# A bias add of the last image on VectorE instead of GpSimd, a frequency table stored in pairs, and two loads in the other order

## The chip, the core and the metric

The kernel runs on one core of one Trainium2 chip. Time is the device time of one execution in microseconds (us). A core has TensorE (PE, matmuls; PEld is its weight load), VectorE (DVE), ScalarE (ACT), GpSimd (POOL) and SyncE (SP, which here only issues transfers). Each executes its own list of instructions in order, and they wait for each other by semaphores. Transfers run on 16 DMA engines; ACT issues some of them too.

## The reference

The input x has 8 images of 128 x 128 pixels with 96 channels. One layer is computed, in two residual steps:

```python
x = x + conv(layernorm(x))        # a global filter in the frequency domain
t = t + ffn(layernorm(t))         # per pixel, 96 -> 384 -> 96
```

`conv` projects 96 to 192 channels, squares the rectified value, takes a two-dimensional FFT, multiplies by a filter, transforms back and projects to 96 channels. The filter is a mix of three stored ones, each interpolated from a small grid over 128 x 65 frequencies; the weights of the mix are a softmax that depends on the image. `ffn` is

```python
h = relu(q_acc(q_acc(q_mul(x) @ q_mul(W1)) + q_mul(b1)))
y = q_acc(q_acc(q_mul(h) @ q_mul(W2)) + q_mul(b2))
```

where q_mul rounds to an 8-bit float (5 exponent bits) and q_acc to fp16. The second bias, b2, is the one that the change moves.

## The kernel before, in words

Each image b runs through three streams. `before` ("a") loads x in blocks of 16 columns for the statistics (`load_x`, line 903) and transposed for the projection, projects, rectifies, squares, transforms along one axis and stores the result Y in device memory. `spectrum` ("s") goes over 33 groups of frequencies: it loads Y and a piece of the table T (`load_t`, line 1134), weighs T by the image's softmax on GpSimd (tw), builds the filter and the spectrum on PE, multiplies them on VectorE, mixes channels and transforms back on PE, and stores V. `after` ("c") goes over 8 blocks of 16 columns, each of four units (q) of 4 columns, 32 units in all: `load_v` (line 1386) loads the block of x into `t` and the block of V into `vin`; `last` (PE, pk) is the last inverse transform, `residual` (DVE) adds it to t; then come the statistics (bn_stats on DVE, `variance` and `rest` on POOL, a root on ACT and a reciprocal on DVE), the normalised and quantised z, its transposition (pz on PE, zT on ACT), `first` (PE, ph), `accumulated` (ACT, y in fp16), `biased` (DVE, y + b1), `hidden` (h), `second` (PE, po), `put` (ACT, o in fp16), the second bias, the sum with t, and the store.

T is a tensor in device memory, filled at the start of the run (`row_store`, line 783): 2 halves x 64 rows x 65 frequencies x 192 channels in fp32. A group g uses the frequencies g+1 and g+33.

Up to the seventh image the second bias and the sum are done for a whole block on GpSimd (`bias`, `add_up`: 128x1536, L1495 and L1498). For the last image they are done unit by unit: `bias_part` (L1502, 128x384) and `add_part` (L1506), both on GpSimd before. For that image the normalisation also differs: `centre` subtracts the mean on GpSimd (L1416, into vin), `norm` multiplies on VectorE (L1423, z), and `hidden` is split between ACT (two thirds, L1473) and DVE (one third, L1471).

The order of the work is not left to a scheduler of the chip. Every piece is recorded by `at` with what it needs; `in_order` (line 472) goes through them with a cost for each kind (COST), with a place in time for each (WINDOWS by stream and image, OFFSETS by kind), and for some kinds of VectorE with an exclusion against GpSimd (SHARED). It writes one list per engine, and at the end each instruction is tied to the one before it on its engine (PINNED), so that the lists stand as written. `keep_warm` (line 636) puts matmuls on zeros (L642, "warm") ahead of some pieces on PE, as many as WARM says for the image and piece. Two pieces of the end matter below: `second` of a unit is ordered after the four `add_part` of the block two before, because o has two buffers, and `load_v` of a block after the store of the block five before, because t has five.

The transfers are issued by SP in the order in which `in_order` has put them; `load_v` issues two, `load_x` one, `load_t` one.

Of the kernel before, what the change touches and what calls it, by code (L numbers as in the profile page):

```python
# [43 lines left out]
MED = 192  # L44
# [23 lines left out]
WINDOWS = {  # L68
    "a": ((-1497.5, 329.4), (863.1, 879.3), (649, 969.5), (584.6, 116.7), (49.5, 721.3), (910.6, 691.7), (1676.3, 504.2), (2001.5, 512.8)),
    "s": ((23.8, 262.2), (71, 1106.2), (630.6, 311.7), (754.9, 352.4), (629.3, 734.8), (-354.6, 114.4), (713.6, 123.4), (2091.2, 75.3)),  # L70
    "c": ((1077.8, 438.5), (962.8, 173.4), (1098.5, 307), (1684.2, 504.4), (1984, 366.6), (2465, 69), (2244, 686.2), (2737, 1205.9)),
}
OFFSETS = {
    "a_context": -91.63,
# [51 lines left out]
    "a_variance": 33.04,  # L126
    "a_variance_1": 33.04,
    "c_accumulated": -189.82,
    "c_accumulated_8": 12.18,
    "c_add_part_8": -199.88,  # L130
    "c_add_up": -72,
    "c_bias": -208.64,
    "c_bias_part_8": 1548.65,
    "c_biased": -131.17,
    "c_biased_8": 271.9,
    "c_centre_8": 49.3,
    "c_first": -9.52,
    "c_first_8": -1055.54,
    "c_hidden": -106.95,
    "c_hidden_2_8": -971.11,  # L140
    "c_hidden_v_8": 73.57,
    "c_inverse": -43.31,
    "c_inverse_8": 194.44,
    "c_last": -159.45,
    "c_last_8": 67.27,
    "c_load_v": -76.92,
    "c_load_v_8": -73.71,
    "c_measure": 212.19,
    "c_measure_8": -31.7,
    "c_norm_8": -808.2,  # L150
    "c_put8": -62.08,
    "c_put8_8": 1012.64,
    "c_quantise": 163.76,
    "c_quantise_v": 259.01,
    "c_residual": -74.18,
    "c_residual_8": -2157.99,
    "c_rest": -211.52,
    "c_rest_8": 83.6,
    "c_root": 122.39,
    "c_root_8": -0.97,  # L160
    "c_second": -134.92,
    "c_second_8": -285.01,
    "c_store": 507.71,
    "c_store_8": -1049.43,
    "c_store_part_8": 881.57,
    "c_turn8": -248.18,
    "c_turn8_8": 72.63,
    "c_turned8": 91.19,
    "c_turned8_8": 922.13,
    "c_variance": -140.17,  # L170
    "c_variance_8": 771.21,
    "s_alone_t": 386.55,
    "s_alone_x": 26.26,
    "s_alone_z": 209.95,
# [22 lines left out]
    ('a', 1): {('project', 0, 0): 4, ('transform', 0, 2): 7, ('transform', 1, 2): 4},  # L197
    ('s', 1): {('along_w', 1): 6, ('invert', 9, 0): 4},
    ('c', 1): {('second', 7): 4},
    ('c', 6): {('first', 12, 0): 4, ('second', 22): 12, ('second', 23): 8, ('first', 24, 0): 3, ('first', 25, 0): 6, ('second', 26): 3, ('first', 27, 0): 6, ('second', 27): 4, ('first', 28, 0): 3, ('second', 28): 10, ('turn8', 7, 1): 6, ('first', 29, 0): 3, ('second', 29): 11},  # L200
    ('s', 7): {('along_w', 4): 3, ('invert', 15, 0): 5},
    ('c', 7): {('last', 0, 0): 3, ('first', 2, 0): 17, ('first', 3, 0): 17, ('first', 5, 0): 11, ('first', 6, 0): 7, ('second', 6): 8, ('first', 7, 0): 8, ('turn8', 2, 0): 12, ('first', 10, 0): 15, ('first', 12, 0): 20, ('first', 14, 0): 15, ('second', 14): 8, ('first', 15, 0): 8, ('second', 15): 15, ('first', 18, 0): 15, ('first', 22, 0): 3, ('second', 22): 7, ('first', 23, 0): 15, ('last', 6, 0): 3, ('turn8', 6, 0): 11, ('first', 26, 0): 15, ('first', 27, 0): 14, ('last', 7, 0): 6, ('first', 28, 0): 7, ('first', 29, 0): 7, ('first', 30, 0): 7, ('second', 30): 8, ('first', 31, 0): 8, ('second', 31): 11},
}

PINNED = (
# [87 lines left out]
    "s_load_y": (SP, 0.9, 1.25),  # L293
    "s_load_t": (SP, 0.65, 0.576),
    "c_load_v": (SP, 2.1, 4.736),
    "c_bias_part": (POOL, 0.84, 0),
    "c_add_part": (POOL, 0.82, 0),
    "c_store_part": (SP, 0.4, 0.48),
    "s_store_v": (ACT, 0.375, 1),
    "c_store": (SP, 0.4, 1.92),  # L300
# [1 line left out]
    "_load_scales": (SP, 2.4, 5),  # L302
}
QUARTER = {"s_along_w", "s_filters_of", "s_mix_low", "s_mix"}
SHARED = {"a_scale", "c_biased", "a_rate_n", "a_rate_v3", "c_quantise_v", "c_hidden_v"}
INSTR = {
    "a_project": 8, "a_transform": 4, "a_rate_p0": 4, "a_rate_p1": 8, "a_rate_p2": 12, "s_along_w": 96,
    "s_filters_of": 24, "s_mix_low": 96, "s_mix": 96, "s_invert": 4, "c_last": 4, "c_turn8": 8, "c_turn32": 16,
# [37 lines left out]
    return [(NG - 1, 0), (NG, 0), (NG - 1, 1), (NG, 1), (NG + 1, 0)] if r == 0 else [(NG - 1, 0), (NG + 1, 0), (NG - 1, 1)]  # L346


def _constants():

    n = np.arange(128)
    angle = 2 * np.pi * (np.outer(np.arange(L), n) % 128) / 128
    cos, sin = np.cos(angle), np.sin(angle)
    sin[0] = sin[L - 1] = 0.0
    norm = 1 / np.sqrt(128.0)

    middle = 2 * np.pi * np.outer(np.arange(64) - 63.5, np.arange(L)) / 128
    half = np.cos(middle), np.sin(middle)
    half[0][:, L - 1] = 0.0
    turn = np.pi * (127 * np.arange(L) % 256) / 128  # L360
    turn = np.cos(turn), -np.sin(turn)
    weight = np.full((L, 1), 2.0)
    weight[0] = weight[L - 1] = 1.0

    rows = []
    for g in range(NG):
        k = g + 1
        rows += [k, k + 32, 64 + k, 96 + k]
    rows += [32, 96, 0, 64]

    turned = []
    for p in range(NP):
        for cs in range(2):
            for r in range(2):
                for g in (2 * p, 2 * p + 1):
                    turned.append(g + 1 + 32 * r + 64 * cs if g < NG or r == 0 else 64 * (1 - cs))
    out = {
        "F1": np.concatenate([cos, sin[1:-1]])[rows].T * norm,
        "F2": np.concatenate([np.stack([half[0], -half[0]], 1), np.stack([half[1], half[1]], 1)]) * norm,
        "GL": np.concatenate([weight * cos, -2 * sin[1:-1]]) * norm,  # L380
        "GM": np.concatenate([-cos[:1], -2 * sin[1:-1], -cos[L - 1 :], -2 * cos[1:-1]]) * norm,
        "GK": np.concatenate([cos, -sin[1:-1]])[turned] * norm,
        "CEN": np.eye(C) - 1 / C,
    }
    order = list(range(L)) + [H - k for k in range(1, L - 1)]
    rw = np.zeros((2, 64, 2, L))
    sel = np.zeros((64, NS), np.float32)

    def turned_by(i, row, c, share):

        rw[i, row, c] += share * turn[0]
        rw[i, row, 1 - c] += share * turn[1] * (1 if c == 0 else -1)

    for s, (hh, ww) in enumerate(SCALE_HW):
        m = _resize_mat(hh, H)
        out[f"RH{s}"] = m[order].T
        even, odd = (m[:L] + m[-np.arange(L) % H]) / 2, (m[:L] - m[-np.arange(L) % H]) / 2
        pr, pi, qr, qi = even.copy(), odd.copy(), even.copy(), -odd
        for k in (0, L - 1):
            pi[k], qr[k], qi[k] = 0.0, 0.0, -m[k]  # L400
        out[f"RE{s}"] = np.concatenate([pr, pi, qr, qi]).T
        w = _resize_mat(ww, L).T
        ends = np.zeros((2, L))
        ends[0, 0] = ends[1, L - 1] = 1.0
        w[:, 0] = w[:, L - 1] = 0.0
        for i in range(2):
            for c in range(2):
                for n in range(ww):
                    turned_by(i, c * NW + WOFF[s] + n, c, w[n])
                    sel[c * NW + WOFF[s] + n, s] = 1.0  # L410
            for e in range(2):
                for q in range(2):
                    row = R + 4 * s + 2 * q + e
                    turned_by(i, row, q ^ i, ends[e] * (1 if q == i else -1) * (-1 if i and e else 1))
                    sel[row, s] = 1.0
    rw[1, :, 1] *= -1
    out["RW"], out["SEL"] = rw.reshape(128, 2 * L), np.concatenate([sel, sel])
    return {k: np.ascontiguousarray(v, dtype=np.float32) for k, v in out.items()}
# [183 lines left out]
def metaformer_kernel(ctx: ExitStack, tc: tile.TileContext, a: dict, out: bass.AP):  # L602
# [132 lines left out]
    def filters(sp):  # L735
# [47 lines left out]
        def row_store(i, s):  # L783
            (_, c, w0, n), tk = next(p for p in pieces[i] if p[0] == s), pts.pop((i, s))
            r0 = c * NW + WOFF[s] + w0
            nc.sync.dma_start(out=T[0, r0 : r0 + n, :, :].rearrange("r k m -> k r m"), in_=tk[:L, :n, :])
            nc.sync.dma_start(out=T[1, r0 : r0 + n, 1 : L - 1, :].rearrange("r k m -> k r m"), in_=tk[L:, :n, :])

        w1f = sp.tile([C, HID], F32, name="w1f")
        w2f = sp.tile([128, NHC, C], F32, name="w2f")  # L790
# [103 lines left out]
    def before(b, t0, P):  # L894
# [8 lines left out]
        def load_x(blk):  # L903
            if blk == 0:
                kept["gacc"] = pa.tile([C, NU // 2], F32, name="gacc", tag="gacc")
            xb = pa.tile([128, WB, C], F32, name="xb", tag="xb")
            nc.sync.dma_start(out=xb, in_=xw[b, blk])
            kept["x", blk] = xb

        def measure(blk, q):  # L910
# [202 lines left out]
    def spectrum(b, t0, P):  # L1113
# [20 lines left out]
        def load_t(g):  # L1134
            tb = kept["tb", g] = psp.tile([128, 2 * MED], F32, name="tb", tag="tb")
            to = tb.rearrange("p (k m) -> p k m", k=2)
            if g < NG:
                nc.sync.dma_start(out=to, in_=T[:, :, g + 1 : g + 34 : 32, :].rearrange("s r k m -> (s r) k m"))
            elif g == NG:
                both = T[:, :, 32, :].rearrange("s r m -> (s r) m").unsqueeze(1).to_broadcast([128, 2, MED])  # L1140
                nc.sync.dma_start(out=to, in_=both)
            else:
                nc.sync.dma_start(out=to[:64, :, :], in_=T[0, :, 0 : L : L - 1, :])

        def weigh(g):
            p = slice(0, 128 if g <= NG else 64)
# [232 lines left out]
    def after(b, t0, P):  # L1379
# [6 lines left out]
        def load_v(blk):  # L1386
            assert kept_v[b] == 16
            w = slice(blk * WB, (blk + 1) * WB)
            xr = kept["t", blk] = pools["c"].tile([128, WB, C], F32, name="t", tag="t", bufs=5)
            vin = kept["vin", blk] = pools["c"].tile([128, WB, C], F32, name="vin", tag="vin")  # L1390
            nc.sync.dma_start(out=xr, in_=x[b, :, w, :])
            nc.sync.dma_start(out=vin, in_=V[b][w, :, :].rearrange("w j c -> j w c"))

        def last(blk, q):
            w = slice(q * QW, (q + 1) * QW)
# [103 lines left out]

        def bias_part(blk, q):  # L1500
            o = kept["o", blk][:, q * QW : (q + 1) * QW, :]
            nc.gpsimd.tensor_tensor(o, o, b2q.unsqueeze(1).to_broadcast([128, QW, C]), ALU.add)  # L1502

        def add_part(blk, q):
            w = slice(q * QW, (q + 1) * QW)
# [146 lines left out]
```

## Time and profile before

| | us |
|---|---|
| median of three runs | 2722.2 |
| lowest, highest | 2716.2, 2723.7 |
| the profiled execution, its own time | 2713.8 |
| its span, first to last instruction | 2712.0 |
| mean granted TensorE clock | 0.976 of full speed |
| PE, DVE, ACT, POOL busy | 2503.9, 2258.1, 2126.5, 1746.2 |
| bytes moved, mean rate | 621 MB, 229 GB/s |
| DMA packets | 506,545 |

All sums below are made against the profiled execution. In a list of groups, a row gives line, engine, operation, out<-in with partitions x elements and type, count, then busy time in us and the mean duration of one in ns, then the idle time of the engine just before them and what ended most of it. In a list in order of time, the columns are the start in us, the duration in us, engine, line, operation and tiles, and in brackets the idle time before it. An instruction that stands still on its engine while it holds it counts as busy. Busy time of a matmul is modelled, so a busy PE is not a PE at its peak.

### The profile page before, as it was taken

The numbers are of one execution on the slowest core, as the hardware profiler recorded it, in microseconds if no ns is written. First come the engines' busy times: TensorE is split into PE (matmuls) and PEld (weight loads), VectorE is DVE, ScalarE is ACT, GpSimd is POOL, SyncE is SP. The second block draws the span as 40 slices with busy tenths as digits, with TensorE's granted clock in tenths as the row PEclk, the third lists the DMA queues.
The fourth block names the chain that finished last, engine by engine and source line by source line (L and its number), as shares of the span: only waits on it lengthen the run. The fifth ranks groups of instructions, "written<-read, shape, count | busy, mean of one in ns | idle before, by whom it ended". The sixth has DMA issues, their size and how long they took to land.

```text
span 2712.0 us, 92856 instructions
## 1 busy us (share of the span) xinstructions
PE 2503.9 (92%) x37552; PEld 1796.8 (66%) x37552; DVE 2258.1 (83%) x5405; ACT 2126.5 (78%) x4300; POOL 1746.2 (64%) x2591
## 2 busy tenths in 40 slices
PE   6999999999989999999999999999999998889898
PEld 3556677766767766666667677766666776666454
DVE  5568688789788798889898998988888988998767
ACT  2455565558999799977898789889989987879877
POOL 2235445456667476775877667767766776777688
PEclk8899999999999999999999999999999999999999
DMA  8889889898976996679768888786758674774442
GB/s 226 258 257 286 248 266 295 265 274 250 273 223 206 292 279 194 188 245 284 222 196 265 261 254 270 248 263 209 233 182 259 202 226 132 232 217 141 131 135 75
DMA packets 506545, 621.24 MB, mean 229 GB/s; under 512 B 165246, under 2 KB 440599, under 8 KB 506091
## 3 DMA queue, kind: packets, MB, share of 16 engines
q1 hardware_dynamic: 418050, 464.28, 58.6%
q10 hardware_dynamic: 88064, 151.02, 15.4%
q8 instruction: 296, 4.85, 0.8%
q14 instruction: 135, 1.10, 0.1%
HBM read 407.03 MB, written 208.16 MB: 227 GB/s over the span
## 4 chain that ended last, share of the span: by engine, by line
PE 56%; ACT 17%; DMA 9%; DVE 9%; issue 5%; POOL 3%; SPq 1%; ACTq 0%; POOLq 0%; DVEq 0%
PE px L941 11%; PE py L970 9%; PE pv L1260 7%; PE pf L1179 5%; PE pz L1164 5%; PE pg L1301 5%; ACT y L1460 4%; PE pk L1397 4%; ACT h L1473 4%; DMA vin<-Vd 3%; PE ph L1453 3%; PE po L1480 3%; ACT z L1433 2%; DMA zT<-in_xT 2%; PE warm L642 2%
## 5 line engine op out<-in xcount | busy, mean ns | idle before, releaser
L941 PE MATMUL px<-W1S,zT 97*128 97x240 f32 x2048 | 495.7, 377 | 10.1 <-DVE yst L982 5.3
L941 PEld LDWEIGHTS px<-W1S,zT 97*128 97x128 f32 x2048 | 387.9, 194 | 119.4 <-DVE yst L982 10.5
L1149 POOL TENSOR_TENSOR tw<-tb,r 128x384 f32<-128x384 f32 (+1 forms) x264 | 288.7, 1093 | 265.2 <-PE pf L1179 152.2
L1460 ACT CAST y<-ph 128x512 f16<-128x512 f32 x768 | 418.0, 606 | 47.6 <-PE ph L1453 25.2
L970 PE MATMUL py<-X,F 128*128 128x384 f32 x1024 | 432.1, 513 | 17.2 <-DVE yst L982 7.8
L952 ACT ACTIVATE rl<-px 128x480 f32<-128x480 f32 x512 | 291.7, 581 | 117.7 <-PE px L941 85.9
L1473 ACT ACTIVATE h<-y 128x1536 fp8e5<-128x1536 f16 (+1 forms) x256 | 372.3, 1454 | 12.0 <-DVE y L1464 11.7
L1464 DVE TENSOR_TENSOR y<-y,b1q 128x1536 f16<-128x1536 f16 x256 | 306.5, 1197 | 79.5 <-ACT y L1460 78.6
L1260 PE MATMUL pv<-w2C,xf 64*64 64x96 f32 x9264 | 318.8, 247 | 30.9 <-issue 27.0
L1433 ACT ACTIVATE z<-t,ln_m,ln_r 128x96 fp8e5<-128x96 f32 x784 | 337.1, 479 | 6.7 <-POOL ln_m L885 3.6
L966 POOL TENSOR_TENSOR sacc<-sacc,rl 128x192 f32<-128x192 f32 x248 | 168.9, 681 | 259.1 <-ACT rl L952 240.5
L1260 PEld LDWEIGHTS pv<-w2C,xf 64*64 64x64 f32 x9264 | 276.2, 135 | 63.0 <-issue 47.0
L982 DVE TENSOR_TENSOR yst<-py,yb 128x384 f32<-128x384 f32 x512 | 261.0, 545 | 62.5 <-ACT rl L952 19.0
L1208 DVE TENSOR_TENSOR t<-d,pf 128x780 f32<-128x780 f32 x256 | 245.2, 958 | 68.7 <-PE pf L1179 40.9
L1202 DVE TENSOR_TENSOR d<-pz,sr 128x390 f32<-128x390 f32 x512 | 264.6, 553 | 30.0 <-ACT sr L1195 29.4
L1222 POOL TENSOR_TENSOR xf<-t 128x390 f32<-128x390 f32 x256 | 238.6, 932 | 69.9 <-DVE t L1208 49.5
L1179 PE MATMUL pf<-RW,tw 64*128 64x130 f32 x3120 | 251.7, 291 | 18.6 <-DVE t L1213 7.4
L1164 PE MATMUL pz<-F,yt 64*64 64x65 f32 x12480 | 252.3, 223 | 17.1 <-issue 9.3
L1164 PEld LDWEIGHTS pz<-F,yt 64*64 64x64 f32 x12480 | 217.1, 136 | 62.8 <-issue 18.4
L1179 PEld LDWEIGHTS pf<-RW,tw 64*128 64x128 f32 x3120 | 200.4, 188 | 81.8 <-issue 35.9
L1453 PE MATMUL ph<-zT,W1q 96*128 96x512 fp8e5 x768 | 237.4, 382 | 17.5 <-DVE t L1403 4.0
L970 PEld LDWEIGHTS py<-X,F 128*128 128x128 f32 x1024 | 183.7, 194 | 95.7 <-issue 20.4
(137 smaller groups left out, 5220.2 us busy)
## 6 DMA issues: line engine op xcount, KB each, us to landing
Yd<-yst ACTq DMA_DIRECT2D x256, 384.0 KB
yt<-Yd SPq DMA_DIRECT2D x248, 384.0 KB
xb<-in_xw SPq DMA_DIRECT2D x64, 768.0 KB
zT<-in_xT SPq DMA_DIRECT2D x128, 384.0 KB
rB<-Rd SPq DMA_DIRECT2D x128, 384.0 KB
tb<-T SPq DMA_DIRECT2D x256, 192.0 KB
Vd<-gst ACTq DMA_DIRECT2D x128, 384.0 KB
t<-in_x SPq DMA_DIRECT2D x64, 768.0 KB
```

What stands on the lines that cost most here:

```text
L941: nc.tensor.matmul(px[:, i * (MED + SCTX) : (i + 1) * (MED + SCTX)], lhsT=zTs[(b * NU // 2 + u // 2) % NZT][:, QW * (u % 2) + i0 + i, :], ...
L952: nc.scalar.activation(kept["rl", u][:, i0 : i0 + 2, :].rearrange("h w m -> h (w m)"), kept.pop(("px", u, i0)), AF.Relu)
L970: nc.tensor.matmul(py, lhsT=F1, rhs=kept["X", u][:, i0 : i0 + 2, :].rearrange("h w m -> h (w m)"), start=True, stop=True)
L1149: nc.gpsimd.tensor_tensor(tw[p, :].rearrange("p (q k m) -> p k q m", q=3, k=2), tb[p, :].rearrange(order, k=2, q=3), rates[b][p, :].rearra ...
L1164: nc.tensor.matmul(halves[i][64 * k : 64 * k + 64, c * L : (c + 1) * L], lhsT=kept["yt", g][rows, 2 * cs + k, 64 * q : 64 * q + 64], rhs=F ...
L1179: nc.tensor.matmul(pf[:, s, q * 2 * L : (q + 1) * 2 * L], lhsT=tw[p, 128 * q : 128 * q + 128], rhs=RW[p, :], start=True, stop=True,)
L1260: nc.tensor.matmul(kept["pv", p, r][half, i * C : (i + 1) * C], lhsT=kept["xf", g][rows, k, q, half], rhs=(w2N if k == 1 and h == 1 else w ...
L1433: nc.scalar.activation(z, t, AF.Identity, bias=m, scale=r, saturate=False)
L1453: nc.tensor.matmul(kept["ph", u, n], lhsT=W1q[:, n * 128 : (n + 1) * 128], rhs=kept["zT", u], start=True, stop=True)
L1460: nc.scalar.copy(kept["y", u][:, n, :], kept.pop(("ph", u, n)))
L1464: nc.vector.tensor_tensor(y, y, b1q, ALU.add)
L1473: nc.scalar.activation(h, y, AF.Relu, saturate=False)
```

## The change

Five things are changed, and the places by which `in_order` writes the order of the last two images' streams.

1. `bias_part` is executed by VectorE. Its cost is set to 0.38 and that of `add_part` from 0.82 to 0.94, and `c_bias_part` joins SHARED.
2. The frequencies of T are stored in the order 1, 33, 2, 34, ..., 31, 63, 32, 0, 64 (a new function `_order`), in the matrices that fill it as well, so that `load_t` of a group reads two neighbours: 1536 bytes in one run for each of 128 rows, where it read two runs of 768.
3. `load_v` issues the load of vin ahead of that of t.
4. The first block of the first image is loaded for the statistics in two halves of 8 columns.
5. New places for the last image's `after` (OFFSETS ending in _8 and two entries of WINDOWS), and new counts of warm matmuls: 97 instead of 79 in the `after` of the image before it, 16 instead of 8 in the last spectrum, 264 instead of 301 in the last `after`; all others are unchanged, 499 instead of 510 in the whole run.

```diff
-    "c": (..., (2244, 686.2), (2737, 1205.9)),
+    "c": (..., (2164.4, 738), (2245.7, 323.4)),
...
-    "c_add_part_8": -199.88,
+    "c_add_part_8": -362.05,
...
-    "c_bias_part_8": 1548.65,
+    "c_bias_part_8": 4124.83,
...
-    "c_bias_part": (POOL, 0.84, 0),
-    "c_add_part": (POOL, 0.82, 0),
+    "c_bias_part": (DVE, 0.38, 0),
+    "c_add_part": (POOL, 0.94, 0),
...
-SHARED = {"a_scale", "c_biased", "a_rate_n", "a_rate_v3", "c_quantise_v", "c_hidden_v"}
+SHARED = {"a_scale", "c_biased", "a_rate_n", "a_rate_v3", "c_quantise_v", "c_hidden_v", "c_bias_part"}
...
+def _order():
+
+    return [k for g in range(NG) for k in (g + 1, g + 33)] + [32, 0, 64]
...
-    order = list(range(L)) + [H - k for k in range(1, L - 1)]
+    order = _order()
+    low = order[:L]
+    order += [H - k for k in low[: L - 2]]
...
-        out[f"RE{s}"] = np.concatenate([pr, pi, qr, qi]).T
+        out[f"RE{s}"] = np.concatenate([pr[low], pi[low], qr[low], qi[low]]).T
...
-            nc.sync.dma_start(out=T[1, r0 : r0 + n, 1 : L - 1, :].rearrange("r k m -> k r m"), in_=tk[L:, :n, :])
+            nc.sync.dma_start(out=T[1, r0 : r0 + n, : L - 2, :].rearrange("r k m -> k r m"), in_=tk[L:, :n, :])
...
-            nc.sync.dma_start(out=xb, in_=xw[b, blk])
+            for n in range(0, WB, WB if b or blk else HB):
+                part = slice(n, n + (WB if b or blk else HB))
+                nc.sync.dma_start(out=xb[:, part, :], in_=xw[b, blk, :, part, :])
...
-                nc.sync.dma_start(out=to, in_=T[:, :, g + 1 : g + 34 : 32, :].rearrange("s r k m -> (s r) k m"))
+                nc.sync.dma_start(out=to, in_=T[:, :, 2 * g : 2 * g + 2, :].rearrange("s r k m -> (s r) k m"))
...
             vin = kept["vin", blk] = pools["c"].tile([128, WB, C], F32, name="vin", tag="vin")
+            nc.sync.dma_start(out=vin, in_=V[b][w, :, :].rearrange("w j c -> j w c"))
             nc.sync.dma_start(out=xr, in_=x[b, :, w, :])
-            nc.sync.dma_start(out=vin, in_=V[b][w, :, :].rearrange("w j c -> j w c"))
...
-            nc.gpsimd.tensor_tensor(o, o, b2q.unsqueeze(1).to_broadcast([128, QW, C]), ALU.add)
+            nc.vector.tensor_tensor(o, o, b2q.unsqueeze(1).to_broadcast([128, QW, C]), ALU.add)
```

Left out are the other new offsets of the last image, the two loads of T for its last three frequencies (they follow the new order), and the list of WARM.

## The prediction

> **What bounds the kernel now.** I read the page first: the shares of the engines, and the chain that ended last. Then stretches of the end, the groups of the last 134 us, the engines' rows in order of time, and the waits.
>
> ```profile
> PE 2503.9 (92%) x37552; PEld 1796.8 (66%) x37552; DVE 2258.1 (83%) x5405; ACT 2126.5 (78%) x4300; POOL 1746.2 (64%) x2591
> ...
> PE 56%; ACT 17%; DMA 9%; DVE 9%; issue 5%; POOL 3%; SPq 1%; ACTq 0%; POOLq 0%; DVEq 0%
> ```
>
> Over the whole run TensorE sets the pace; GpSimd, which the change relieves, is 3% of the chain. But that is an average over stages. The stretches (columns: length, then busy us of PE, PEld, DVE, ACT, POOL, then clock and DMA share) show the end apart:
>
> ```profile
> 2370.00:2515.00 145.00, 127.53 (x2763) 93.97 (x2763) 124.87 (x267) 122.61 (x260) 108.01 (x130) 0.98 0.57 173
> 2515.00:2575.00 60.00, 50.22 (x336) 25.72 (x334) 43.69 (x85) 51.92 (x100) 39.35 (x51) 1.00 0.46 139
> 2575.00:2640.00 65.00, 63.68 (x439) 35.04 (x436) 47.53 (x103) 47.84 (x87) 52.07 (x73) 0.97 0.39 123
> 2640.00:2680.00 40.00, 36.99 (x269) 20.46 (x267) 31.72 (x65) 32.66 (x62) 35.78 (x47) 1.00 0.31 99
> ```
>
> From 2575 us on, the last image is alone. POOL is busy 80 to 89% there, but PE 98 and 92%: it is filled with the matmuls on zeros of `keep_warm`, which stand in its order like any other work. The groups of 2575 to 2709 us (busy us, mean ns) give their weight and the price of what is moved:
>
> ```profile
> L642 PE MATMUL warm<-zeros 128*64 128x512 bf16 x281 | 67.8, 388 | 0.3
> L1506 POOL TENSOR_TENSOR t<-t,o 128x384 f32<-128x384 f32 x32 | 39.8, 1242 | 2.5
> L1502 POOL TENSOR_TENSOR o<-o,b2q 128x384 f16<-128x384 f16 x32 | 36.1, 1128 | 8.7 <-ACT o L1491 8.7
> ```
>
> In order of time, GpSimd and VectorE are seen to take turns:
>
> ```profile
> 2685.61 1.08 POOL L1502 TENSOR_TENSOR o<-o,b2q 128x384 f16<-128x384 f16 x1
> 2685.85 1.66 DVE L1464 TENSOR_TENSOR y<-y,b1q 128x1536 f16<-128x1536 f16 x1
> 2686.77 1.50 POOL L1506 TENSOR_TENSOR t<-t,o 128x384 f32<-128x384 f32 x1
> 2687.62 0.95 DVE L1471 TENSOR_SCALAR h<-y 128x512 fp8e5<-128x512 f16 x1
> ```
>
> The undisturbed durations (minima, or common values, of the same rows) are 0.90, 0.89, 0.91 and 0.41 us. Each of the four runs about as much longer as its neighbour on the other engine still had to go: one at a time.
>
> For the transfers, the waits (total us, times, longest):
>
> ```profile
> PE pk L1397 <- DMA vin<-Vd: 8.0, 8, 2.0
> POOL tw L1149 <- DMA tb<-T: 15.1, 11, 4.2
> SPq L1391 <- DMA out<-t: 35.6, 17, 4.8
> SPq L1392 <- DVE z L1423: 58.9, 6, 18.4
> ```
>
> **What the Trainium skill says.** "SBUF — State Buffer", section "Who interferes with whom": VectorE and GpSimd share a port pair that is an exclusive lock; a VectorE instruction with two inputs in SBUF contends with a GpSimd instruction that reads SBUF, and one blocks wholly. The four rows above agree. So the bias stays a user of that lock after it is moved. "VectorE: DVE Perf Modes", section "The perf-mode tier table": tensor_tensor on 16-bit data in SBUF runs at two elements a cycle, on fp32 at one. The trace agrees: 1536 fp16 elements take 0.89 us at best, 768 fp32 ones 0.97. "DMA: Bandwidth & Descriptors", section "Why small descriptors are slow": each packet carries a fixed overhead besides its bytes; the trace agrees in sign (below).
>
> **The change, part by part** (sums against the profiled execution: 2713.8 us, span 2712.0; the median of the runs shown is 2722.2, so 8.4 more).
>
> *Bias.* 32 GpSimd instructions go: 36.1 us with their waits, 32 x 0.90 = 28.9 without. VectorE gets 32 of 128x384. The y row's 0.89 us less 1536/2/0.96 GHz = 0.80 leaves 0.09 fixed, so 0.20 + 0.09 = 0.29 us each, 9.3 us in all (an estimate from that page's rate); at one element a cycle 0.49 and 15.7 us. I take 0.29, since y has the same types. The lock is held 28.9 - 9.3 = 19.6 us less (13.2 at the slow rate). VectorE lost, in 2480 to 2712 us, (1.258 - 0.89) x 47 = 17 us in y and (0.735 - 0.41) x 32 = 10 us in h; as half of the GpSimd work beside them goes, some 14 of these 27 come back, and pay for the 9.3 and for the waits of the 32 new ones. So VectorE stays as loaded; GpSimd is relieved.
>
> *Order and fill of the end.* The orders of the two kernels are the same on PE, DVE, ACT and POOL, warm matmuls too, until about 2330 to 2400 us; then they are written anew by the new places. Real work is the same, but the counts of warm matmuls change: last image 301 to 264, image before it 79 to 97, its spectrum 8 to 16. One costs 3.45/15 to 3.89/17 = 0.22 to 0.23 us (rows of 15 and 17 in a run): 37 fewer are 8 us, where PE is 92 to 98% busy; 26 more are 6 us, of which most fall in 2370 to 2575 us, where PE idles 17.5 + 9.8 us. I charge 2 of the 6, and -8 + 2 = -6. I don't credit the 19.6 us of lock on top: with PE full, the fill holds the pace, and the freed lock can only remove what PE still idled. For that I take -1: the last unit ends with ACT's put, one add of 0.3 instead of 0.9, then the fp32 add. Bounds: 0 (the idle moves elsewhere) to -19.6. In the last 25 us ACT alone (1.43 + 1.05 + 0.37 + 0.49 = 3.3 us a unit, the rows there lie 3.2 us apart) allows no more.
>
> *vin before t.* 64 times the load from Vd goes ahead of the load of x on SP. One issue (0.43 us) is passed, and the wait for the store of the out-tile (35.6 us in 17 waits) no longer stands ahead of vin; vin also starts ahead of 768 KB of x. At the 229 GB/s of the page those are 3.4 us. PE's 8.0 us of waits for vin therefore go; `residual` needs both loads, so VectorE waits for t instead, about as late as vin was. I take -3 of the 8. In the last image the wait of 58.9 us (vin's buffer, freed by z) now stands ahead of t. What is queued behind it on SP stays behind it, but t lands some 3 us after vin instead of before. Only blocks whose pk follows within 6 us feel it: one (vin issued at 2553.5, pk at 2558.8) and perhaps the first: +1. Bounds -8 to +6.
>
> *Table T side by side.* 248 loads take 128 runs of 1536 B instead of 256 of 768 B: 31,744 packets fewer of 506,545. Queue 1: 58.6% x 16 x 2712 / 418,050 = 60.8 ns for a mean of 1,111 B; queue 10: 75.9 ns for 1,715 B. The line through both has 33 ns at zero bytes, so 31,744 x 33 / 16 = 65 us of DMA time, 2.4% of the span, at most (an estimate; zero if time goes by bytes alone). The loads run ahead (POOL waits 15.1 us for tb, and isn't the bound there); the cover is the second buffer, and without it 65/248 = 0.26 us a load would count. I take -1; bounds -6 to 0. The stores of T and the matrices that fill it keep their sizes.
>
> *First block in halves.* One issue of 0.39 us more, the first statistics up to 1.3 us earlier (half of 2.65); both hidden, since GpSimd reaches `rest` of block 0 at 13.7 us only, behind the weights, that wait for `bn` until 11.4. 0; bounds -1.3 to +0.4.
>
> Sum: -6 - 1 - 3 + 1 - 1 = -10 us: 2703.8 beside 2713.8, and 2712 as a median.
>
> **Rivals.**
> *The lock was the pace.* For it: POOL at 89% in 2640 to 2680, DVE held up 27 us. Against it: PE is full too. Then 19.6 us come off instead of the 7 of bias and fill: about 2700.
> *It hides.* PE's idle grows by what the fill gives up, and t is late where vin was: 2715 to 2728.
> *The bias comes in bursts, and the end waits (slower).* In the new order VectorE adds no bias until its twelfth y, then 8 of them round a z, with seven fp32 adds on GpSimd in a row; behind them PE has 24 warm matmuls (5.3 us) and two `second` units at once. `second` of unit 8 waits for the four adds of block 0: four of 0.29 and four of 0.91, taking turns with y, z and h, are 5 us undisturbed and some 9 with the turns (z 1.9, h 0.95, y 1.66 as above). From 5.3 us on, PE and ACT stand still. Three such places (24, 8 and 10 warm matmuls, some 4, 7 and 7 us short) lose 18, against the 10: +8 to +12, about 2732. For it: VectorE executes in order, and a pair of z that took 7.60 us together already stops ACT for 6.3 us. Against it: `second` trails by several units, which ACT can use.
>
> **How the numbers follow.** Chances: the forecast's own case (2704 to 2718) 0.42; lock 0.2; hidden 0.2; bursts 0.18. A difference of 0.3% is 8 us, about what this measurement tells from none. Faster: 0.2 of the lock and 0.36 of the forecast's 0.42: 0.56. Same: 0.06 and the hidden 0.2, 0.26. Slower: 0.18. The range runs from the lock with vin's and the table's full bounds (2692) to the middle of the bursts (2731). The likeliest one's own range is 2704 to 2718.
>
> **What would show it.** L1502 on DVE x32 at 0.29 us minimum and about 0.6 mean; POOL's share in the last 130 us down from 85 to about 60%; PE still over 90% busy there, with about 265 warm matmuls; `pk <- vin` near 0, and a new wait of DVE `t` for the DMA of t; about 31,700 fewer packets. If PE falls below 88% in the end, the bursts were right or the fill did not hold the pace; if the first 2300 us move by over 6 us, I have misjudged the loads.

## The result, and the profile after

The changed kernel took 2703.65 us (median of 9 executions, 2687.39 to 2710.5), the kernel before 2716.2 us beside it (median of 9, 2710.04 to 2723.72). The ratio over all these executions is 0.9941, 95% interval 0.9915 to 0.9967: faster by 0.6%, or 16 us, with 9 to 23 us inside the interval (the two medians by themselves are 12.6 us apart). The interval lies just beyond the 0.3% that the prediction took as the limit of this measurement. Measured once more in a later series it was 0.9938 (0.9908 to 0.9969). The profiled execution took 2710.5 us, its span is 2708.3.

The page of the changed kernel, from which three lines answer to those shown of before (shares of the engines, the busiest transfer queue, the chain that ended last):

```profile
PE 2508.2 (93%) x37541; PEld 1800.9 (66%) x37541; DVE 2265.9 (84%) x5437; ACT 2128.7 (79%) x4300; POOL 1703.0 (63%) x2559
...
q1 hardware_dynamic: 385938, 464.28, 57.7%
...
PE 17%; ACT 8%; DVE 4%; issue 2%; POOL 1%; DMA 0%; ACTq 0%; POOLq 0%; DVEq 0%
```

VectorE has 32 instructions more and GpSimd 32 fewer. The queue has 32,112 packets fewer than before (418,050). This chain is followed back over a third of the span only, so its shares don't compare with those of before.

The same four stretches as before (columns: length, then busy us of PE, PEld, DVE, ACT, POOL, then clock and DMA share):

```profile
2370.00:2515.00 145.00, 135.20 (x2886) 97.42 (x2886) 128.20 (x271) 123.90 (x264) 114.71 (x135) 0.99 0.58 184
2515.00:2575.00 60.00, 57.53 (x392) 30.69 (x391) 43.84 (x89) 58.17 (x113) 41.62 (x58) 1.00 0.44 132
2575.00:2640.00 65.00, 56.37 (x389) 31.02 (x388) 52.86 (x111) 49.09 (x90) 31.74 (x45) 0.95 0.36 110
2640.00:2680.00 40.00, 35.12 (x244) 19.10 (x243) 35.10 (x72) 27.18 (x51) 30.32 (x44) 1.00 0.26 90
```

In the first two rows PE is now 93 and 96% full, where it was 88 and 84% before (127.53 of 145, 50.22 of 60). From 2575 to 2640 us it is the other way round: 98% before, 87% now. POOL fell there from 80% to 49%. The groups of 2575 to 2709 us (busy us, mean ns):

```profile
L649 PE MATMUL warm<-zeros 128*64 128x512 bf16 x228 | 54.9, 385 | 0.3
L1515 POOL TENSOR_TENSOR t<-t,o 128x384 f32<-128x384 f32 x32 | 33.7, 1067 | 18.7 <-DVE o L1511 9.6 <-ACT y L1469 3.7 <-ACT h L1482 3.0
L1511 DVE TENSOR_TENSOR o<-o,b2q 128x384 f16<-128x384 f16 x32 | 19.2, 628 | 2.1 <-ACT o L1500 2.1
```

The bias costs VectorE 19.2 us where it cost GpSimd 36.1. Its fastest instruction took 292 ns, its mean is 628. GpSimd, which had no idle time before its sums, now waits 18.7 us for them.

Executions of one kernel differ by more than the change is worth, so I measured two intervals inside each trace. ScalarE issues 128 stores of V, and up to the 17th from the last the order of PE, DVE, ACT and POOL is the same in the two kernels. **Lead-in** is from that store to the last store of V; **tail** is from there to the end of the span. The two rows of before:

```profile
2301.54:2515.30 213.76, 189.30 (x4014) 139.01 (x4013) 186.11 (x390) 178.99 (x376) 158.81 (x185) 0.98 0.63 191
2515.30:2712.00 196.70, 176.67 (x1227) 95.35 (x1225) 142.44 (x267) 154.48 (x285) 155.30 (x193) 0.98 0.36 115
```

and of after:

```profile
2308.51:2512.70 204.19, 190.66 (x4015) 137.06 (x4014) 186.34 (x392) 175.39 (x369) 160.41 (x185) 0.99 0.65 202
2512.70:2708.30 195.60, 173.78 (x1218) 94.21 (x1214) 147.64 (x297) 157.56 (x292) 115.89 (x161) 0.98 0.35 113
```

The lead-in is 9.6 us shorter, the tail 1.1: 10.7 together. PE idles 24.5 us of the old lead-in and 13.5 of the new one. Some of the lead-in's work was put off: ScalarE has 3.6 us less there and 3.1 more in the tail. So the gain appears ahead of the tail, where no bias was moved, and the tail is no longer for it. The experiments ask which part of the change pays for which.

### The profile page after: what moved, and what is told of

Same layout as the page of the kernel before. It is cut to its first block, busy times and chain, and to the rows that moved or that the text cites. A ratio compares the mean times of both kernels' runs of the same rounds, so it can differ in the third digit from the quotient of the medians.

```text
span 2708.3 us, 92884 instructions
## 1 busy us (share of the span) xinstructions
PE 2508.2 (93%) x37541; PEld 1800.9 (66%) x37541; DVE 2265.9 (84%) x5437; ACT 2128.7 (79%) x4300; POOL 1703.0 (63%) x2559
## 3 DMA queue, kind: packets, MB, share of 16 engines
q1 hardware_dynamic: 385938, 464.28, 57.7%
## 5 line engine op out<-in xcount | busy, mean ns | idle before, releaser
L950 PEld LDWEIGHTS px<-W1S,zT 97*128 97x128 f32 x2048 | 388.3, 194 | 121.9 <-DVE yst L991 10.7
L991 DVE TENSOR_TENSOR yst<-py,yb 128x384 f32<-128x384 f32 x512 | 261.0, 544 | 61.0 <-ACT rl L961 24.5
L1217 DVE TENSOR_TENSOR t<-d,pf 128x780 f32<-128x780 f32 x256 | 245.0, 957 | 63.7 <-PE pf L1188 37.9
L1222 DVE TENSOR_TENSOR t<-d,pf 128x780 f32<-128x780 f32 x256 | 244.9, 957 | 0.0
```

What stands on the lines that cost most here:

```text
L950: nc.tensor.matmul(px[:, i * (MED + SCTX) : (i + 1) * (MED + SCTX)], lhsT=zTs[(b * NU // 2 + u // 2) % NZT][:, QW * (u % 2) + i0 + i, :], ...
```

## The experiments

All ratios are to the kernel before, run beside on the same chip. Lead-in and tail are from one profile each. Kernels with the same instructions in the lead-in gave 201.6 to 205.3 us in the new order and 212.6 to 217.5 in the old, so it tells 5 us and not 2 (the two longest of the old order, 214.7 and 217.5, ran at a granted clock of 0.95 there, the other three at 0.98). The tails of the three kernels that have the changed one's whole end (after, after again, all but the transfers) lie within 0.4 us. "Fill" stands for the warm matmuls of the last image.

| kernel | ratio | 95% interval | lead-in | tail |
|---|---|---|---|---|
| before | 1 | | 213.8 | 196.7 |
| after | 0.9941 | 0.9915 to 0.9967 | 204.2 | 195.6 |
| after, again | 0.9938 | 0.9908 to 0.9969 | 203.9 | 195.9 |
| transfers alone | 0.9989 | 0.9966 to 1.0012 | 214.7 | 197.2 |
| all but the transfers | 0.9973 | 0.9952 to 0.9994 | 205.3 | 195.5 |
| bias alone, old order | 1.0007 | 0.9978 to 1.0037 | 213.6 | 195.1 |
| after, bias on GpSimd | 1.0008 | 0.9983 to 1.0033 | 203.1 | 210.6 |
| place of the seventh image alone | 1.0031 | 1.0011 to 1.0051 | 204.0 | 212.6 |
| before, no fill | 0.9998 | 0.9976 to 1.0019 | 212.6 | 194.1 |
| bias alone, no fill | 0.9978 | 0.9958 to 0.9998 | 217.5 | 188.7 |
| after, no fill | 0.9928 | 0.9909 to 0.9946 | 201.6 | 192.3 |
| after, bias earlier | 1.0077 | 1.0050 to 1.0103 | 203.6 | 231.1 |
| after, bias earlier, no fill | 0.9972 | 0.9953 to 0.9991 | 203.5 | 203.7 |
| after, no warm matmul at all | 0.9926 | 0.9895 to 0.9958 | 199.7 | 195.0 |

### The transfers apart from the rest

The first kernel is the one before with the three changes to transfers (T in pairs, vin ahead of t, the first block in halves) and nothing else; the second is the changed kernel without them. The edit of the first, its core:

```diff
-                nc.sync.dma_start(out=to, in_=T[:, :, g + 1 : g + 34 : 32, :].rearrange("s r k m -> (s r) k m"))
+                nc.sync.dma_start(out=to, in_=T[:, :, 2 * g : 2 * g + 2, :].rearrange("s r k m -> (s r) k m"))
...
+            nc.sync.dma_start(out=vin, in_=V[b][w, :, :].rearrange("w j c -> j w c"))
             nc.sync.dma_start(out=xr, in_=x[b, :, w, :])
-            nc.sync.dma_start(out=vin, in_=V[b][w, :, :].rearrange("w j c -> j w c"))
```

> The kernel before with the three transfer edits alone (table in pairs, vin ahead of t, first block in halves); bias, order and fill of the end as before. My account: -3 us (-2 for vin, -1 for the table), a ratio of 0.998 to 1.000; waits of PE for vin go from 8 us to under 1, DMA packets from 506,545 to about 474,400. Rival 'the loads carry the gain': -10 to -13 us, ratio about 0.996.

> The changed kernel without its three transfer edits: bias on VectorE with the new order and the new counts of warm matmuls. My account: -7 us, ratio about 0.997; from the last store of V to the end about 195 us. Rival 'the loads carry the gain': -2 us, ratio about 0.999. Rival 'the lock was the pace': -20 us, ratio 0.993.

Measured: the transfers alone 0.9989 (0.9966 to 1.0012), which is 3 us less, with anything from 9 less to 3 more; the rest without them 0.9973 (0.9952 to 0.9994), 7 us less. By the two intervals in the trace the transfers give nothing in the end (411.9 us against 410.5), and the rest gives 9.6 of the 10.7. The end carries most of the gain; what the transfers add can't be told from none. The two ratios multiplied make 0.9962, while the whole change measured 0.9941 and 0.9938: some 6 us that the intervals leave room for and that no run places. Of the waits of the changed kernel (total us, times, longest), those for the table and for x read

```profile
POOL tw L1158 <- DMA tb<-T: 6.3, 3, 3.4
...
DVE t L1412 <- DMA t<-in_x: 3.4, 3, 1.4
```

against 15.1 for the table before; PE's 8.0 us for vin are gone from the list, and VectorE's wait for t is new. The exchange of vin for t is the work of the transfers: with all but the transfers PE still waits 6.6 us for vin, and with the transfers alone it doesn't, and VectorE waits 4.2 us for t. The table's shorter wait isn't shown to be: it is 11.1 us in the kernel with all but the transfers, which has the old layout, and 10.2 in the one with the new layout alone.

### The bias and the order, each without the other

Three kernels. In the first, only the engine of the bias changes and every list keeps its old order (the new instruction stands in VectorE's list by the old place):

```diff
-            nc.gpsimd.tensor_tensor(o, o, b2q.unsqueeze(1).to_broadcast([128, QW, C]), ALU.add)
+            nc.vector.tensor_tensor(o, o, b2q.unsqueeze(1).to_broadcast([128, QW, C]), ALU.add)
```

> The kernel before with one word changed: the 32 adds of the bias are on VectorE, each where it stood in the old order, with the old 301 warm matmuls in the last image. My account (the fill holds the pace): -1 to -3 us, ratio 0.999; PE still above 93% busy from 2575 us on. Rival 'the lock was the pace': 19.6 us less of it shows at once, -15 to -20 us, ratio about 0.993.

In the second, the changed kernel gets its bias back on GpSimd, at its new place:

```diff
-            nc.vector.tensor_tensor(o, o, b2q.unsqueeze(1).to_broadcast([128, QW, C]), ALU.add)
+            nc.gpsimd.tensor_tensor(o, o, b2q.unsqueeze(1).to_broadcast([128, QW, C]), ALU.add)
```

> The changed kernel with the 32 adds back on GpSimd, in the new order. My account: the new order puts eight of them in a row ahead of seven sums, so that block 0 is released 4 x 0.6 us later and the two later bursts likewise; +5 to +10 us against the changed kernel, ratio to the kernel before 0.998 to 1.001. Rival 'the lock was the pace': +20 us against the changed kernel, ratio 1.001 to 1.003. If it is as fast as the changed kernel, engine and lock don't matter and only order and fill do.

In the third, the kernel before gets only the new place of the seventh image's `after`, with the warm matmuls that go with it:

```diff
-    "c": (..., (2244, 686.2), (2737, 1205.9)),
+    "c": (..., (2164.4, 738), (2737, 1205.9)),
```

> The kernel before with the new place and fill of the seventh image's `after` and of the last spectrum alone; bias on GpSimd, the last image's places and fill and the loads as before. If that place brings the gain by itself: from the 17th-last store of V to the last one about 204 us instead of 214, from there to the end 197 to 201 (one unit more is left over), in all -6 to -10 us. If it only lends it to the end, which the cheaper bias pays back: 204 and about 207, in all 0.

Measured: 1.0007, 1.0008 and 1.0031. Neither the bias alone nor the order alone shows a gain (the ends of their intervals leave room for 6 and 5 us), and the seventh image's new place alone loses 0.3%. Set out by lead-in plus tail, in us (the new order here is the changed kernel's, with its transfers):

| | bias on GpSimd | bias on VectorE |
|---|---|---|
| old order | 213.8 + 196.7 = 410.5 | 213.6 + 195.1 = 408.7 |
| new order | 203.1 + 210.6 = 413.7 | 204.2 + 195.6 = 399.8 |

Read down: the new place of the seventh image takes 10 us off the lead-in with either engine, and by itself makes it 204.0. Read across: the bias is worth 1.8 us in the old order and 13.9 in the new one (15.0 in the tail). By the ratios (1.0008 against 0.9941) it is 18 us in the new order, nearest to the +20 of the lock rival and above the 5 to 10 of my own account. The place of the seventh image puts work off, which a tail with the bias on GpSimd pays back with 14 us and more (210.6 and, with the old places of the last image, 212.6, against 196.7); on VectorE it doesn't. The bias on VectorE was not tried with the seventh image's new place and the last image's old ones, so which of the two new places it needs stays open.

What the freed time turns into is seen in the rows. In the old order, groups of the tail:

```profile
L1506 POOL TENSOR_TENSOR t<-t,o 128x384 f32<-128x384 f32 x32 | 36.7, 1150 | 50.0 <-DVE o L1502 37.5 <-ACT zT L1449 7.4 <-ACT y L1460 2.8
...
L1502 DVE TENSOR_TENSOR o<-o,b2q 128x384 f16<-128x384 f16 x32 | 11.9, 373 | 4.6 <-ACT o L1491 4.6
```

GpSimd is relieved of 36 us and then waits 50 us ahead of its sums, 37.5 of them for the bias, which stands in VectorE's list where GpSimd used to reach it. In the new order with the bias left on GpSimd, the tail and waits of it:

```profile
2501.27:2711.90 210.63, 177.50 (x1218) 96.07 (x1214) 139.13 (x265) 157.92 (x292) 153.34 (x193) 0.95 0.33 105
```

```profile
DVE y L1473 <- ACT y L1469: 34.7, 19, 7.6
...
DVE z L1432 <- POOL ln_r L662: 10.3, 6, 3.5
ACT o L1500 <- POOL t L1515: 8.6, 2, 8.0
```

These are 25.4, 5.2 and 3.9 us in the changed kernel: VectorE waits longer for ScalarE's y and for GpSimd, and ScalarE for GpSimd, whose busy time in the tail is 153 us against 116. VectorE's own instructions also take longer beside it: y 1352 against 1312 ns, z 1473 against 1386, h 726 against 561, over 42, 16 and 32 of them 8.4 us. How much of the 15 us is that turn-taking and how much is GpSimd's list being too long, these runs don't separate.

### Does the fill hold the pace?

The prediction's largest term, -8 us, priced 37 warm matmuls at 0.22 us. Taking away all of the last image's must then give 301 x 0.22 = 66 us, unless something else holds. These matmuls multiply zeros and nothing reads what they give, so the kernels called "no fill" leave out no work of the reference. The edit is the same in three kernels, one line of WARM:

```diff
-    ('c', 7): {...},
```

> The kernel before without the 301 warm matmuls of the last image (their results are used nowhere). If the fill holds the pace of the end: from the last store of V to the end 5 to 15 us less than 197. If GpSimd and the lock hold it: the same 197 within 2 us. If the clock needs the fill: longer, at a lower granted clock.

> The same without fill, and with the bias on VectorE in the old order. If the fill had hidden the freed lock: 10 to 20 us less from the last store of V to the end than the run without fill and with the bias on GpSimd. If the lock isn't what the old order waits for: within 3 us of it.

> The changed kernel without the 264 warm matmuls of the last image (their results are used nowhere). If the fill holds the pace: 5 to 15 us less than 195.6 from the last store of V to the end. If the bursts of adds do: within 3 us, with the same waits of PE for h behind `second`.

Measured: 0.9998 (0.9976 to 1.0019) for the kernel before, its tail 2.6 us shorter. So leaving out 301 matmuls, with all that follows from it, is worth 0.5 us, and at most 6.5 us at the end of the interval, 0.02 us each. In the changed kernel leaving out 264 of them is worth some 3 us (0.9928 against 0.9941, with intervals that overlap; the tail is 3.3 us shorter, and only 0.6 us in the last kernel of the table, which has no warm matmul in its tail at all). Both tails lie near the 2 and 3 us that were expected if something other than the fill holds the pace. The tail of before without its fill, as a stretch:

```profile
2532.49:2726.60 194.11, 134.69 (x926) 77.88 (x924) 142.00 (x267) 154.83 (x285) 157.32 (x193) 0.75 0.37 116
```

and the waits there:

```profile
PEld L1479 <- ACT h L1472: 52.4, 34, 4.4
PE po L1479 <- ACT h L1472: 33.0, 23, 3.9
```

PE is busy for 135 of 194 us instead of 177 of 197; what the fill had covered comes out as waits for ScalarE's h. One thing else changed with it: the granted clock of this tail fell from 0.98 to 0.75, and ph took 465 ns instead of 378. Less its warm matmuls (91.0 us of busy time before, 18.6 now) PE is busy for some 116 us instead of 86. So the run doesn't say what the fill costs at an unchanged clock. It does say that PE gave up 42 us of busy time, the slower clock included, and the tail 2.6: a good part of PE's 98% in the last image was idle time with a cover on it, and PE's busy time did not hold the pace there.

The bias alone without fill has the shortest tail of all, 188.7 us, 5.4 less than before without fill: perhaps in the old order too the moved bias is worth something once PE's list gives way. That is between the two outcomes foreseen (10 to 20 us, or within 3), and from one profile of each. As a whole it is 0.9978 (0.9958 to 0.9998), an interval that overlaps that of before without fill.

### The burst, and a fill that doesn't fit

The prediction's slower rival was that the bias comes in bursts. In the changed kernel, in order of time (start us, duration us, engine, line, operation, tiles, idle before):

```profile
2604.93 5.41 PE L649 MATMUL warm<-zeros 128*64 128x512 bf16 x24
...
2612.95 4.29 DVE L1511 TENSOR_TENSOR o<-o,b2q 128x384 f16<-128x384 f16 x5
...
2614.15 4.91 POOL L1515 TENSOR_TENSOR t<-t,o 128x384 f32<-128x384 f32 x5 [0.36 <-DVE o L1511]
...
2616.07 0.48 ACT L1500 CAST o<-po 128x384 f16<-128x384 f32 x1 [3.91 <-POOL t L1515]
...
2618.35 0.98 PE L1489 MATMUL po<-W2q,h 128*128 128x96 fp8e5 x10 [4.61 <-DVE h L1480]
```

The burst is there: five adds, which take 0.35 us each where nothing holds them up, take 4.29, turn by turn with five sums on GpSimd, h stands behind them in VectorE's list, ScalarE waits 3.9 us and PE 4.6. This is again what the Trainium skill, "SBUF — State Buffer", section "Who interferes with whom", says of the lock between the two engines. The question was whether spreading the adds would give these 4.6 us back. The place of the bias was set earlier, which writes VectorE's list anew: the first block's adds come between the y instead of around a z. Then the same without the fill:

```diff
-    "c_bias_part_8": 4124.83,
+    "c_bias_part_8": 0,
```

> The changed kernel with an earlier place for the bias, so that the adds of the first block are spread between the y and no longer stand in one burst around a z. If the burst costs what PE's stand of 4.6 us behind it shows: the end from the last store of V falls by 3 to 5 us to about 191, ratio 0.9925. If that stand is covered, like the stalls that the fill covers: 195 to 196 us, ratio 0.994. If the early adds make VectorE wait for ScalarE's o and hold up the y behind them: above 198.

> The same without the 264 matmuls on zeros of the last image (they do no work of the result). If the fill is only idle time: 2 to 4 us less than with it, ratio 0.991 to 0.993. If the lower granted clock without the fill costs what PE's longer matmuls take: no less than with it.

Beside them ran the changed kernel again, and the changed kernel without any warm matmul:

> The changed kernel once more, beside the three that follow, so that they can be set against it on one chip. Expected: 0.994 of before (0.992 to 0.997); from the last store of V to the end 195 to 196 us.

> The changed kernel without any of its 499 matmuls on zeros, the last image's 264 and 235 elsewhere (113 of them in the seventh image and the last spectrum). If a warm matmul costs its 0.22 us where PE is over 90% busy: the 113 give 25 us, ratio 0.984. If they fill idle time there too: as without the last image's alone, 0.992 to 0.994. If the clock that they keep up is needed where PE is the bound: the stretch ahead of the last store of V grows from 204 us by 5 to 20, ratio 0.995 to 1.000.

The earlier place is slower, 1.0077 (1.0050 to 1.0103), with a tail of 231.1 us, and that was expected of it only if VectorE waits for ScalarE's o and early adds hold up the y. But most of it is something else: without the fill it is 0.9972 (0.9953 to 0.9991), tail 203.7. Here the 264 warm matmuls cost 27 us of tail, 0.10 us each, some eight times what they cost in the changed kernel. With the fill, the stretch in the middle of the tail, two rows of it in order of time, and waits of the tail:

```profile
2551.44:2616.44 65.00, 53.54 (x342) 28.15 (x340) 37.98 (x78) 37.89 (x69) 24.36 (x34) 0.87 0.27 86
```

```profile
2585.20 5.12 PE L649 MATMUL warm<-zeros 128*64 128x512 bf16 x13
...
2590.81 1.56 ACT L1469 CAST y<-ph 128x512 f16<-128x512 f32 x3 [4.85 <-PE ph L1462]
```

```profile
ACT y L1469 <- PE ph L1462: 15.8, 9, 4.8
...
ACT o L1500 <- PE po L1489: 15.0, 11, 4.0
```

Without it, waits of the tail:

```profile
ACT y L1468 <- PE ph L1461: 5.0, 7, 2.9
```

With the fill ScalarE and VectorE are busy for only 38 of these 65 us, because ScalarE waits for ph and po, which stand behind warm matmuls on PE, as in the two rows; the counts were written for another order. The granted clock is lower as well, 0.87 in this stretch, and these 13 warm matmuls take 0.39 us each instead of 0.22; how much of the 27 us is the clock's part isn't separated. Without fill those 15.8 us are 5.0, and po's 15.0 are 8.9. So "a warm matmul is free" holds where the counts fit the order's own gaps, and not in general. What remains without the fill, 203.7 against 192.3 us, says that the earlier place is worse by itself. There GpSimd's sums wait 31.6 us for the bias, against 6.0, while VectorE waits only 3.3 us for ScalarE's o, so the reason that the expectation gave isn't what the trace shows. The list differs in more than the burst, so what the burst alone costs stays open.

Without any of the 499 warm matmuls the changed kernel took 0.9926 (0.9895 to 0.9958). That is the lowest ratio of the study, with the last image's fill gone 0.9928; both are faster than before, and neither is told apart from the changed kernel itself. The lead-in of 199.7 us, where 30 warm matmuls fewer stand on a PE that is 93% busy, hints at a gain there; one profile doesn't show it.

## Why the prediction was right in size, and where its reasons failed

The forecast was -10 us, faster; measured are -0.6% (16 us of the 2716) and -10.7 us between two profiles. As a time the forecast was 2712, likeliest from 2704 to 2718; the measured 2703.65 lies just below the lower edge of that. The direction and the size were right, for a reason that the sum didn't contain, and that is luck.

*Order and fill of the end (-6).* This step failed, in both its halves. "37 fewer are 8 us, where PE is 92 to 98% busy" takes a busy share as a bound; in the kernel before, 301 fewer are 0.5 us, the lower clock that came with it included. And the 26 more, "of which most fall in 2370 to 2575 us, where PE idles", were charged at +2, while exactly there the new place of the seventh image gained 10 us of lead-in, with 18 of the 26 in it: PE's idle time in the lead-in went from 24.5 to 13.5 us. I priced the order by its count of warm matmuls and not by the stretch from 2370 to 2515 us, where PE had 17.5 us of idle time in plain view.

*Bias and lock (-1, bounds 0 to -19.6).* What fell is "with PE full, the fill holds the pace". The moved bias is worth 15.0 us of tail in the new order. That is inside the bounds and nearer to the 19.6 of the lock, though the shorter list of GpSimd is in it too; I took the wrong end. In the old order it is worth 1.6 us of tail, near the -1 taken, but because GpSimd then waits for it.

*The price of the bias.* 0.29 us undisturbed and 0.6 as a mean: measured 292 ns at the least and 628 as a mean, but 292 to 294 in three of the 32 only; in the old order all 32 take 344 ns or more. The 0.09 us fixed came from the fastest y of the whole run (0.89), while in the last image the fastest y takes 0.93. "So VectorE stays as loaded": half right. With only the engine changed, the 27 us lost in y and h did come back by half, as forecast: y from 1262 to 1065 ns and h from 735 to 526, 15 us, and VectorE's busy time in the tail fell from 142.4 to 134.8. In the new order it grew to 147.6: h came back (561 ns), y did not (1312), and z, which I hadn't counted, gave 8.6 us (1948 to 1386 ns), most of that by the order, since it is 1473 there with the bias on GpSimd. Of the four rows that I set beside the rule of the lock, the last, h, has one input and isn't covered by the rule as I gave it; it was held up all the same (0.95 us against 0.41).

*GpSimd and PE shares.* GpSimd's share from 2575 us to the end was to fall from 85 to about 60%: it is 73.3 of 133.3 us, 55%. PE was to stay above 90%, and below 88% would mean the bursts or a fill that doesn't hold the pace: it is 87% from 2575 to 2680 us, and both are seen.

*vin and T (-3 +1 -1).* vin's wait went as foreseen, from 8.0 us to none in the list, with 3.4 us of VectorE's for t in its place. The table's went from 15.1 to 6.3, but by 4 of these us with the old layout too. Queue 1 has 32,112 packets fewer where 31,744 were counted. Together the transfers measured -3 us with an interval from -9 to +3, so the sign isn't shown. The 65 us of transfer time were not reached: the queue's share is 57.7 to 58.6% of 16 engines' span in the six kernels with the old packets and 56.7 to 58.2% in the eight with the new, on average 0.5% less, some 14 us, which is no more than kernels with the same packets differ by. The mark "if the first 2300 us move by over 6 us" was no use: with the same order up to there, the 17th store from the last fell anywhere from 2288 to 2320 us.

*The rivals.* "The lock was the pace" was nearest to the mechanism, in the new order only. "It hides" is what the bias does in the old order. "Bursts" happened at one of the three places, and the order still came out ahead: PE's 4.6 us stand in this order and its gains exceed what they cost, which no run measured alone.

## What to carry to other kernels

A busy share that contains filler doesn't tell the bound: take the filler away first, in the profile or in a run, before pricing work by how busy an engine is, and look whether the clock moved with it. Where an order is written by hand, moving work to another engine and the order are one change: here neither showed a gain without the other, and together, with the transfers, they gave 0.6%. And filler belongs to the order for which it was counted; carry it over to another order and it can cost 1%.

## What the runs showed of the hardware that was not expected

Without the fill the granted TensorE clock in the last 190 us fell from 0.98 to between 0.75 and 0.78, and single matmuls took longer (ph 384 to 479 ns, po 209 to 238 in the changed kernel), and yet the tail became no longer: 195.6 us with the fill, 192.3 without the last image's and 195.0 without any warm matmul.

The scatter of executions goes with the mean granted clock. Over 75 executions of the kernel before in one series, the clock ranged from 0.969 to 0.982, and the time fell by 2.5 us for each 0.001 that it was higher (correlation -0.80; which of the two follows the other isn't shown). Those at 0.972 or below took 2725 us on average, those at 0.977 or above 2707. That is as wide as the whole effect of this change, and why intervals inside a trace told more than single times.
